# Edge softmax: turning the sum of s_i and mask by a round trip through DRAM and VectorE, one step ahead

## The chip, the cores and the metric

The kernel runs on one core of one Trainium2 chip. The metric is the device time of one execution in microseconds. A core has TensorE (PE: matrix products, and PEld for its weight loads), VectorE (DVE), ScalarE (ACT), GpSimd (POOL) and SyncE (SP), which here issues nearly all DMAs. Each engine works through its own list of instructions in order.

## The reference

Two layers of attention over a graph run on 128 batches of 128 tokens with 512 features. Layer 0 is masked attention with eight heads, and layer 1 is a graph attention whose scores are a sum of two numbers, s_i and s_j, under the same mask:

```python
def _L1_gnn_ref(h, W, a, adj):
    Wh = jnp.matmul(h, W)
    s_i = Wh @ a1
    s_j = Wh @ a2
    e = _leaky(s_i[:, :, None] + s_j[:, None, :])
    e = jnp.where(adj > 0, e, -9e15)
    attention = jax.nn.softmax(e, axis=1)
    h_prime = jnp.einsum('bij,bjf->bif', attention, Wh)
    return _leaky(h_prime)

x = _layernorm(x + _L0_gnn_ref(x, adj, Wq, bq, Wk, bk, Wv, bv, Wo, bo))
x = _layernorm(x + _L1_gnn_ref(x, W, a, adj))
```

The softmax of layer 1 runs over axis 1, the index i. So the tile of scores, made with i on the partitions, has to be turned to bring j onto the partitions and i along the free axis.

## The kernel before

Everything is float32. The batches are taken in groups of four for the products with Wq, Wk and Wv (`products`, each a Strassen scheme of seven part products), in pairs for those with Wo (`LayerZero`) and W (`LayerOne`), and singly for the softmax of layer 0 (`Softmax`) and for layer 1's attention (`Edge`).

One loop runs over steps t = -3 to 123, and then a written plan (`PLAN`) issues what is left of the last batches. In step t the kernel makes layer 0's softmax of batch t, its attention with V of batch t-1, a part of a group's products (`group()`), a pair's products (`pair()`: LayerZero at odd t, LayerOne of batches t-6 and t-5 at even t), and works on the edge softmax of the batches some seven behind. The order of the instructions on each engine is the order in which the code issues them; nothing reorders them.

Seven part products make a Strassen block, in the order of `ORDER`: ("p1", "t0"), ("p5",), ("p6", "t2"), ("p2", "c11"), ("p7", "t3", "c22"), ("p4", "c21"), ("p3", "c12"). Each call of `pair()` or `group()` takes one of these entries. p1, p6, p7 and p4 add into one PSUM bank ("y"), p5 and p3 into "w", and p2 has "x". t0, t2 and t3 are copies of "y" as it stands at that moment, made by ScalarE (pr_t for pairs, L456; st_t for groups, L341 and L345), so the next product into "y" must wait for the copy. c11 and the others are the finished blocks. For LayerOne they are written to `WH` (wh, L770 on VectorE and L768 on ScalarE), whose last column in each half holds s_i (half 0, c11 for the even batch and c21 for the odd one) and s_j (half 1).

The Edge of batch b goes through these methods:

- `sender()` (L796, ScalarE): e = mask + s_i, from the mask tile mf and a column of WH. At the end of step t it is made for batch t-6.
- `turn()` (L800, TensorE): e is turned with the identity into the PSUM tile p_e. It is called in the next step, behind the scores, the softmax's maxima and one `group()`.
- `add()` (L803, ScalarE): s_j is added while the tile is read from PSUM, and e is written back.
- `maxima()` (L808, L810, VectorE), `exp()` (L814, ScalarE), `divide()` (L818, L819, VectorE), then `product()` (p_h, L824, TensorE), `copy()`, `residual()`, `stats()`, `rstd()` (L648 and L650 on GpSimd), `apply()` (L663) and `store()` (L848, SyncE).

In the same step ScalarE makes eight exponentials of layer 0's softmax (`sm.exp`, L550) and eight divides (`sm.divide`, L564); VectorE makes the reciprocals between (`sm.reciprocals`, rs, L560). The middle of the step reads:

```python
            sm.exp(7)
            edge.divide()
            pair()
            sm.reciprocals(1)
            sm.divide(0, 1, 2, 3)
            group()
            sm.divide(4, 5)
            pair()
            sm.divide(6, 7)
```

Then `sm.spread()` writes pa to DRAM (pa_dram, L570) and, once it has landed, fetches it in four pieces as paz (L576), so that blocks of 32 by 32 stand where a transpose of such blocks on VectorE (paT, L585) makes the whole turn. SyncE also fetches batches in blocks (xz, L238), the masks (adj, L487), the residuals (L254) and the weights of V (wv_n, L405, a ring of three buffers), and sends x1 to DRAM (x_dram, L714). On GpSimd, `sum_x` forms the sums xS (L273 to L276) of a group's x at every fourth step, t divisible by 4.

Of the kernel before, what the change touches and what calls it, by code (L numbers as in the profile page):

```python
# [8 lines left out]
F32 = mybir.dt.float32  # L9
# [15 lines left out]
def kernel(  # L25
# [59 lines left out]
    nc = tc.nc  # L85
    B, P, D = x.shape
# [9 lines left out]
    small = ctx.enter_context(tc.tile_pool(name="small", bufs=3))  # L96
    dram = ctx.enter_context(tc.tile_pool(name="dram", bufs=3, space=bass.MemoryType.DRAM))
# [42 lines left out]
    def load_blocks(*args, **kwargs):  # L140
        for load in block_loads(*args, **kwargs):
            load()
# [4 lines left out]
    def right_blocks(t):  # L147

        return [
            lambda: nc.vector.tensor_sub(t[2], t[2], t[0]),  # L150
            lambda: nc.vector.tensor_sub(t[5], t[3], t[2]),
            lambda: nc.vector.tensor_sub(t[4], t[5], t[0]),
            lambda: nc.vector.tensor_sub(t[6], t[1], t[5]),
        ]

    def places(w):
        return [w[:, n] for n in range(7)]

    def columns(w):
        return w[:, 0:2], w[:, 2:4]  # L160
# [72 lines left out]
    def spread(src):  # L233

        z = work.tile([P, 4, P], F32, name="xz", bufs=3)
        block = src.rearrange("(a i) (q e) -> q i a e", i=32, q=4)
        for q in range(4):
            nc.sync.dma_start(z[32 * q : 32 * q + 32], block[q])  # L238
        return z
# [11 lines left out]
    def load_residual(b):  # L251

        X1[b] = work.tile([P, D], F32, name="x1", bufs=7)
        nc.sync.dma_start(X1[b], x[b])  # L254
# [230 lines left out]
    def load_mask(b):  # L485
        MF[b] = small.tile([P, P], I32, name="adj", bufs=2)
        nc.sync.dma_start(MF[b], adj[b])  # L487
# [9 lines left out]
    class Softmax:  # L497
# [27 lines left out]
        def add(self, r):  # L525
            if r == 0:
                self.pa = self.tile("pa", [P, 4, H, 32])
            by_head = self.pa.rearrange("p b h k -> p h b k")
            mf = MF[self.b].rearrange("p (b k) -> p b k", b=4)
            nc.vector.tensor_add(  # L530
                by_head[:, r * NC : (r + 1) * NC],
                self.lg[r].rearrange("p c (b k) -> p c b k", b=4),
                mf.unsqueeze(1).to_broadcast([P, NC, 4, 32]),
            )
# [31 lines left out]
                )  # L566

        def store(self):
            self.d = dram.tile([P, 4, H * 32], F32, name="pa_dram")
            nc.sync.dma_start(self.d, self.pa.rearrange("p b h k -> p b (h k)"))  # L570

        def fetch(self):
            self.paz = self.tile("paz", [P, 4, H * 32])
            block = self.d.rearrange("(a i) b e -> b i a e", i=32)
            for k in range(4):
                nc.sync.dma_start(self.paz[32 * k : 32 * k + 32], block[k])  # L576

        def spread(self):

            self.store()  # L580
            self.fetch()

        def transpose(self):
            self.paT = self.tile("paT", [P, H, P])
# [194 lines left out]
    class Edge:  # L779
# [18 lines left out]
        def turn(self):  # L798
            self.p = psum("p_e")[:, :P]
            nc.tensor.transpose(self.p, self.e, ident)  # L800

        def add(self):
            nc.scalar.activation(self.e, self.p, AF.Identity, bias=self.s[:, 1, :])  # L803

# [46 lines left out]
    def on(b):  # L851
        return 0 <= b < B
# [14 lines left out]
    none = Nothing()  # L867
# [16 lines left out]
    sm = fin = edge = coming = none  # L884
# [66 lines left out]
    END = B - GROUP  # L951

    first_homes = {"pa": lambda shape: work.tile(shape, F32, name="pa", tag="x1T")}
    for t in range(-3, END):
        pair_steps = []
        if t % GROUP == 1 and on(t + 3):
            rest = group_steps
            group_steps, v_pieces, fetch_v = products((t + 3) // GROUP)
            group_steps = rest + group_steps
        if t % 2 == 1 and on(t - 3):  # L960
            pair_steps = zero[(t - 3) // 2] = LayerZero((t - 3) // 2)
            pair_steps = pair_steps.steps()
        if t % 2 == 0 and on(t - 6):
            pair_steps = LayerOne((t - 6) // 2).steps()

        def group(n=1):
            for _ in range(min(n, len(group_steps))):
                group_steps.pop(0)()
            for _ in range(min((3 if t == -3 else 2 if t >= 1 else 1) * n, len(chores))):
                chores.pop(0)()  # L970

        def w1_chores(n):
            for op in [w1_sums.pop(0) for _ in range(n)]:
                op()

        def pair(n=1):
            for _ in range(min(n, len(pair_steps))):
                pair_steps.pop(0)()

        if on(t + 1):  # L980
            load_mask(t + 1)
        if t == 0:
            load_blocks(Wo, columns(wo), nc.sync, spread_rows=False)
            late_chores = right_blocks(places(wo)) + load_bias()
        if t == 1:
            w1_loads, w1_sums = load_w1()
            for chore in late_chores:
                chores += [w1_loads.pop(0), chore]
            chores += w1_loads

        last, sm = sm, Softmax(t, first_homes if t in (0, 2, 4) else None) if on(t) else none
        sm.scores()
        if t % 2 == 1 and on(t - 3):
            zero[(t - 3) // 2].by()
            zero[(t - 3) // 2].bw()
        if later and t > 4:
            later.pop().go_back()
        if t == 5:
            group(2)
        if t < 3:  # L1000
            sm.maxima()
            group(2)
            if on(t - 2):
                load_residual(t - 2)
            if t == 0 and on(GROUP):
                sum_x(1)()
            sm.exp(0, 1, 2, 3)
            last.transpose()
            group()
            sm.reciprocals(0)  # L1010
            sm.exp(4, 5, 6, 7)
            if t == 1:
# [4 lines that stand above are left out]
            sm.divide(4, 5, 6, 7)  # L1017
            if t == 1:
                group()
            if on(t + 1):  # L1020
                mask_float(t + 1)
        elif t == 4:

            layer = later.pop()
            sm.maxima()
            group()
            layer.apply(0)
            load_residual(2)
            if on(8):
                sum_x(2)()  # L1030
            sm.exp(0, 1)
            group()
            sm.exp(2, 3, 4, 5)
            last.transpose()
            group()
            layer.store(1)
            layer.store(0)
            layer.fetch(1)
            layer.fetch(0)
            sm.exp(6, 7)  # L1040
            group()
            sm.reciprocals(0)
            sm.reciprocals(1)
            sm.divide(0, 1, 2, 3, 4, 5, 6, 7)
            mask_float(5)
        else:
            sm.maxima()
            group()
            if t == 5:
                turn_x1(4)  # L1050
                x1_sums()
            edge = coming
            edge.turn()
            edge.add()
            fin.residual()
            if on(t - 2):
                load_residual(t - 2)
            edge.maxima()
            fin.stats()
            fin.rstd()  # L1060
            x1_sums()
            if t % GROUP == 0 and on(t + GROUP):
                sum_x(t // GROUP + 1)()
            pair()
            sm.exp(0, 1, 2, 3)
            edge.exp()
            pair()
            sm.exp(4, 5)
            last.transpose()
            group()  # L1070
            sm.reciprocals(0)
            pair()
            sm.exp(6)
            fin.apply()
            fin.store()
            sm.exp(7)
            edge.divide()
            pair()
            sm.reciprocals(1)
            sm.divide(0, 1, 2, 3)  # L1080
            if t == 3:
                w1_chores(4)
# [4 lines that stand above are left out]
            if on(t + 1):  # L1087
                mask_float(t + 1)
            group()
            if t in (3, 5):  # L1090
                w1_chores(4 if t == 3 else 8)
        sm.spread()
        for b in x_turns(t):
            transpose_x(b)
        for b in x_turns(t + 1):
            load_x(b)
        if on(t + 1):
            mask(t + 1)
        pair(2)
        if t % 2 == 0 and on(t - 6):  # L1100
            turn_x1(t)
        if t not in (0, 4):
            group(21 if t % GROUP == 0 else 1)
        coming = Edge(t - 6) if on(t - 6) and t + 1 < END else none
        coming.sender()
        fin = edge
        fin.product()
        fin.copy()

        last.attend()  # L1110
        last.copy()
        if t % 2 == 0:
            last.sum(0, 1, 2, 3)
# [183 lines left out]
```

## Time and profile before

| what | value |
|---|---|
| runs | 2420.37, 2423.23, 2420.54 us, median 2420.54 |
| profiled execution, own time | 2418.28 us |
| its span | 2416.5 us |
| mean granted TensorE clock | 0.998 |
| PE busy | 2374.0 us, 98% |
| DVE busy | 1802.4 us, 75% |
| ACT busy | 1521.9 us, 63% |
| POOL busy | 812.7 us, 34% |
| DMA queue of SP | 350448 packets, 376.60 MB, 48.8% of 16 engines |
| p_e on PE (L800) | 117 in the loop of 273 ns each, 11 in the plan |
| a step from its first score product to the next one's | about 18.0 us; 19.7 us where t is divisible by 4 |

A line of instructions names the source line, engine, operation, the tiles as out<-in, shapes and count. A busy time is the time in which at least one such instruction runs; matmuls overlap, so the record of one is longer than its share of the engine. "Idle before" is time in which the engine stood still just ahead of the instruction, with what ended it. The chain of waits follows the end of the run back, at each step to what released the instruction.

### The profile page before, as it was taken

The page shows a single profiled execution, that of the slowest core. Times are in us where ns is not written, and L with a number is a line of the kernel's source. Part 1 is how long each engine was busy: PE and PEld are TensorE (multiplying, and loading weights), DVE is VectorE, ACT ScalarE, POOL GpSimd, SP SyncE. Part 2 cuts the span into 40 slices and gives each one's busy share as a digit, 9 for nine tenths or more (in the row PEclk, how much of TensorE's full clock was granted, in tenths as well). Part 3 has the DMA queues.
Part 4 walks back from the last instruction along what each step waited for, and adds up shares of the span by engine and source line. Part 5 has one row for each costly group of instructions (what it writes and reads, how often), then busy time and mean ns, then how long its engine had stood idle before and what let it go on. Part 6 is the DMA issues. An engine that isn't in the chain of part 4 may idle for free.

```text
span 2416.5 us, 43217 instructions
## 1 busy us (share of the span) xinstructions
PE 2374.0 (98%) x13467; PEld 1984.4 (82%) x13467; DVE 1802.4 (75%) x3602; ACT 1521.9 (63%) x5463; POOL 812.7 (34%) x1195
## 2 busy tenths in 40 slices
PE   8899999999999999999999999999999999999996
PEld 7788888888888888888888888888888888888874
DVE  4677787777777777877877777778778777777777
ACT  3566666666666666666666666666666666666685
POOL 1233333233343333332333433333323334333335
PEclk9999999999999999999999999999999999999999
DMA  6554544544545545445445445454454454554453
GB/s 193 176 159 144 168 154 151 178 147 148 170 149 165 163 145 166 148 157 175 142 152 169 152 162 169 136 170 148 160 169 148 153 171 142 166 169 139 149 165 101
DMA packets 351253, 379.88 MB, mean 157 GB/s; under 512 B 38952, under 2 KB 255024, under 8 KB 351024
## 3 DMA queue, kind: packets, MB, share of 16 engines
q1 hardware_dynamic: 350448, 376.60, 48.8%
q8 instruction: 108, 1.77, 0.3%
q14 instruction: 121, 0.99, 0.1%
q10 hardware_dynamic: 576, 0.52, 0.1%
HBM read 240.91 MB, written 136.05 MB: 156 GB/s over the span
## 4 chain that ended last, share of the span: by engine, by line
PE 89%; DMA 3%; DVE 2%; issue 2%; ACT 2%; POOL 1%; SPq 1%; DVEq 0%; POOLq 0%; ACTq 0%
PE st_y L364 26%; PE p_y L445 17%; PE st_w L364 13%; PE p_w L445 8%; PE st_x L364 6%; PE lg L516 5%; PE p_oT L598 5%; PE p_h L824 4%; PE p_x L445 4%; DMA pa_dram<-pa 1%; PE p_e L800 1%; DMA x_dram<-x 1%; DMA wv_n<-wv 0%; DMA paz<-pa_dram 0%; ACT pa L564 0%
## 5 line engine op out<-in xcount | busy, mean ns | idle before, releaser
L550 ACT ACTIVATE pa<-pa,nmax 128x128 f32<-128x128 f32 x1008 | 392.3, 393 | 12.2 <-DVE nmax L539 12.1
L648 POOL TENSOR_SCALAR ve<-mv 128x1 f32<-128x1 f32 x256 | 70.0, 273 | 865.1 <-DVE mv L644 856.6
L564 ACT ACTIVATE pa<-pa,rs 128x128 f32<-128x128 f32 x1008 | 331.0, 394 | 32.6 <-DVE rs L560 29.3
L530 DVE TENSOR_TENSOR pa<-lg,mf 128x512 f32<-128x512 f32 x252 | 162.0, 685 | 160.1 <-PE lg L516 158.3
L273 POOL TENSOR_TENSOR oS<-oT 128x256 f32<-128x256 f32 x63 | 45.8, 727 | 648.8 <-ACT oT L612 648.8
L341 ACT COPY st_t<-st_y 128x512 f32<-128x512 f32 x192 | 110.4, 575 | 154.7 <-PE st_y L364 154.7
L550 ACT ACTIVATION_READ_ACCUMULATOR pa<-pa,nmax 128x1 f32 x1008 | 192.4, 191 | 0.0
L345 ACT ACTIVATE st_t<-st_y,b_cols 128x256 f32<-128x256 f32 x192 | 80.6, 471 | 168.0 <-PE st_y L364 168.0
L650 POOL TENSOR_TENSOR rstd<-ve,mhalf 128x1 f32<-128x1 f32 x256 | 177.0, 691 | 21.3
L598 PEld LDWEIGHTS p_oT<-paT,v 128*64 128x64 f32 x2016 | 107.5, 136 | 91.5 <-issue 91.0
L612 ACT ACTIVATE oT<-p_oT,b_cols 128x128 f32<-128x128 f32 x504 | 144.0, 368 | 55.0 <-PE p_oT L598 54.0
L456 ACT COPY pr_t<-p_y 128x257 f32<-128x257 f32 (+1 forms) x375 | 138.3, 369 | 53.3 <-PE p_y L445 49.6
L585 DVE STREAM_TRANSPOSE paT<-paz 128x1024 f32<-128x1024 f32 x126 | 156.8, 1245 | 15.5 <-DMA paz<-pa_dram 14.3
L539 DVE TENSOR_REDUCE nmax<-pa 128x8 f32<-128x1024 f32 x126 | 153.7, 1220 | 4.4
L516 PE MATMUL lg<-kT,qT 64*128 64x128 f32 x2048 | 148.7, 285 | 0.0
L516 PEld LDWEIGHTS lg<-kT,qT 64*128 64x128 f32 x2048 | 124.2, 187 | 22.9 <-issue 22.9
L598 PE MATMUL p_oT<-paT,v 128*64 128x128 f32 x2016 | 137.9, 279 | 0.0
L445 PE MATMUL p_y<-wo,oT 128*128 128x256 f32 x504 | 129.8, 380 | 1.4 <-ACT pr_t L456 0.8
L445 PE MATMUL p_y<-w,x1S 128*128 128x257 f32 x496 | 128.0, 380 | 1.9 <-ACT pr_t L456 1.9
L445 PE MATMUL p_y<-wo,oS 128*128 128x256 f32 x504 | 129.4, 379 | 0.0
L445 PE MATMUL p_y<-w,x1T 128*128 128x257 f32 x496 | 128.5, 381 | 0.2 <-DVE x1T L243 0.2
L364 PE MATMUL st_y<-xT,wq 128*128 128x256 f32 x512 | 125.8, 389 | 2.5 <-DMA wq<-in_L_gnn_Wq_dram 2.5
(202 smaller groups left out, 5952.1 us busy)
## 6 DMA issues: line engine op xcount, KB each, us to landing
pa_dram<-pa SPq DMA_DIRECT2D x126, 512.0 KB, 2.6
paz<-pa_dram SPq DMA_DIRECT2D x504, 128.0 KB, 2.6
wv_n<-wv SPq DMA_DIRECT2D x224, 256.0 KB, 2.9
x<-in_x_dram SPq DMA_DIRECT2D x128, 256.0 KB, 2.9
x_dram<-x SPq DMA_DIRECT2D x128, 256.0 KB, 2.6
xz<-x_dram SPq DMA_DIRECT2D x512, 64.0 KB, 2.0
xz<-in_x_dram SPq DMA_DIRECT2D x496, 64.0 KB, 2.1
out_dram<-z SPq DMA_DIRECT2D x120, 256.0 KB, 2.5
```

The costliest lines, as they stand in the source:

```text
L364: nc.tensor.matmul(p[:, m, :], lhs, rhs, start=start and m == 0 and kc == 0, stop=True, skip_group_check=True,)
L445: nc.tensor.matmul(p[:, :width], xs()[n][:, kc, :], w[:, PLACE[n], kc, :], start=start and kc == 0, stop=True, skip_group_check=True,)
L456: nc.scalar.copy(t[:, :width], p[:, :width])
L516: nc.tensor.matmul(self.lg[r][:, c, :], q[rows, c, cols], k[rows, c, cols], start=c == 0, stop=True, skip_group_check=True,)
L530: nc.vector.tensor_add(by_head[:, r * NC : (r + 1) * NC], self.lg[r].rearrange("p c (b k) -> p c b k", b=4), mf.unsqueeze(1).to_broadcast( ...
L539: nc.vector.tensor_reduce(self.nmax, by_head, AX.XY, ALU.max, negate=True)
L550: nc.scalar.activation(self.pa[:, :, h, :], self.pa[:, :, h, :], AF.Exp, bias=self.nmax[:, h : h + 1], accum_out=self.sums[:, h : h + 1],)
L564: nc.scalar.activation(self.pa[:, :, h, :], self.pa[:, :, h, :], AF.Copy, scale=self.rs[:, h : h + 1])
L585: nc.vector.transpose(self.paT.rearrange("p h (a i) -> p a h i", i=32), self.paz.rearrange("p a (h k) -> p a h k", k=32),)
L598: nc.tensor.matmul(self.oT[r * HD : (r + 1) * HD, c, :], v[:, h * HD : (h + 1) * HD], self.paT[:, r * NC + c, :], start=c == 0, stop=True, ...
L612: nc.scalar.activation(OT[pair][:, c, h * P : (h + 1) * P], self.oT[:, c, :], AF.Identity, bias=b_cols[:, 1, c : c + 1],)
L650: nc.gpsimd.tensor_tensor(self.r, ve, mhalf, ALU.pow)
```

## The change

`turn()` on TensorE is replaced, in the loop, by three methods. `store_sender()` writes e to DRAM. `fetch_sender()` reads it back in four pieces, each of 32 partitions by 4 by 32 elements, into a tile ez. `turn_blocks()` turns the blocks of 32 by 32 on VectorE into a tile e_turned, on which `add()` and `maxima()` then work.

The sender and the store are made in the middle of the step ahead, between `sm.reciprocals(1)` and the first divides. The four fetches are issued at the end of that step, between the store of pa and its fetches. The turn comes at the start of the next step, directly behind `sm.scores()`. The plan behind the loop keeps `turn()`.

```diff
         def store(self):
             self.d = dram.tile([P, 4, H * 32], F32, name="pa_dram")
             nc.sync.dma_start(self.d, self.pa.rearrange("p b h k -> p b (h k)"))
...
-        def spread(self):
-
-            self.store()
-            self.fetch()
...
             self.p = psum("p_e")[:, :P]
             nc.tensor.transpose(self.p, self.e, ident)
 
+        def store_sender(self):
+            self.d = dram.tile([P, P], F32, name="e_dram")
+            nc.sync.dma_start(self.d, self.e)
+
+        def fetch_sender(self):
+            self.ez = small.tile([P, 4, 32], F32, name="ez", bufs=2)
+            block = self.d.rearrange("(a i) (q e) -> q i a e", i=32, q=4)
+            for q in range(4):
+                nc.sync.dma_start(self.ez[32 * q : 32 * q + 32], block[q])
+
+        def turn_blocks(self):
+
+            self.e = self.p = small.tile([P, P], F32, name="e_turned", bufs=1)
+            nc.vector.transpose(self.e, self.ez.rearrange("p a e -> p (a e)"))
+
         def add(self):
             nc.scalar.activation(self.e, self.p, AF.Identity, bias=self.s[:, 1, :])
...
         sm.scores()
+        coming.turn_blocks()
...
             edge = coming
-            edge.turn()
             edge.add()
             fin.residual()
...
             edge.divide()
             pair()
             sm.reciprocals(1)
+            coming = Edge(t - 6) if on(t - 6) and t + 1 < END else none
+            coming.sender()
+            coming.store_sender()
             sm.divide(0, 1, 2, 3)
...
-        sm.spread()
+        sm.store()
+        if t >= 6:
+            coming.fetch_sender()
+        sm.fetch()
         for b in x_turns(t):
             transpose_x(b)
...
         if t not in (0, 4):
             group(21 if t % GROUP == 0 else 1)
-        coming = Edge(t - 6) if on(t - 6) and t + 1 < END else none
-        coming.sender()
         fin = edge
         fin.product()
         fin.copy()
```

## The prediction

> **What bounds the kernel now.** I read the page's busy shares first, then the chain of waits, then the timeline of single steps, because a share is an average and this change is worth what its own stage makes of it.
>
> ```profile
> PE 2374.0 (98%) x13467; PEld 1984.4 (82%) x13467; DVE 1802.4 (75%) x3602; ACT 1521.9 (63%) x5463; POOL 812.7 (34%) x1195
> ...
> PE 89%; DMA 3%; DVE 2%; issue 2%; ACT 2%; POOL 1%; SPq 1%; DVEq 0%; POOLq 0%; ACTq 0%
> ```
>
> TensorE is busy 98% of the span and is 89% of the chain. From 300 to 2200 us it waits for nothing but four late weight loads (the waits: 2.4 us on wv_n in all). So a product taken off PE pays in full, and a delay elsewhere costs only where it makes PE wait. The chain through step t = 56 (its first score product starts at 1053.65):
>
> ```profile
> 1056.72 0.11 PE p_e L800
> ...
> 1063.76 0.87 PE p_y L445 x4
> 1064.63 1.73 PE st_y L364 x8
> 1066.36 0.87 PE p_y L445 x4
> ```
>
> p_e takes 0.11 us; it has half the columns of an L445 product, so an eighth of a quartet's 0.87: 0.108. The quartets at 1063.76 and 1066.36 (p7 and p4 of LayerOne) add into the same bank, and between them ACT must copy it (pr_t, "t3"). So p4 is the deadline for ACT. The timeline of that place (start, length, engine, line; PE records start 0.17 us ahead of the chain's pieces):
>
> ```profile
> 1061.25 1.27 DVE L663 TENSOR_SCALAR z<-z,mv,rstd 128x512 f32<-128x512 f32 x1
> 1062.25 1.26 ACT L564 ACTIVATE pa<-pa,rs 128x128 f32<-128x128 f32 x4
> 1062.32 1.34 POOL L274 TENSOR_TENSOR xS<-xS,xT 128x512 f32<-128x512 f32 x1
> 1062.63 1.11 DVE L819 TENSOR_SCALAR att<-att,rt 128x128 f32<-128x128 f32 x1
> ...
> 1063.65 0.41 DVE L770 TENSOR_TENSOR wh<-p_x,pr_t 128x257 f32<-128x257 f32 x1
> 1063.79 0.32 SPq L405 DMA_DIRECT2D wv_n<-wv  x1
> ...
> 1064.19 0.69 ACT L564 ACTIVATE pa<-pa,rs 128x128 f32<-128x128 f32 x2 [0.67 <-DVE rs L560]
> ...
> 1064.79 0.35 ACT L456 COPY pr_t<-p_y 128x257 f32<-128x257 f32 x1
> ...
> 1066.19 1.03 PE L445 MATMUL p_y<-w,x1T 128*128 128x257 f32 x4
> ```
>
> The reader is to see three things. wh<-p_x (c11), which holds the s_i of the even batch, is ready only at 1064.06. ACT has by then done four divides. The t3 copy ends at 1065.14, 1.05 us before p4.
>
> **What the skill says.** The Trainium skill's Perfetto Trace Analysis (Tensor Engine Instruction) calls ACT's and DVE's queues "strict FIFO"; the trace agrees (the divides at 1064.19 idle 0.67 us for rs). SBUF — State Buffer (SBUF: two separate sides) says VectorE and GpSimd take their shared ports as an exclusive lock for a whole instruction; here L663 takes 1.27 us beside POOL's xS sums and 0.51 at 1008.10, and L819 1.11 against 0.29 at 1026.37. VectorE: DVE Perf Modes (The three transpose paths) has VectorE turn 32x32 blocks only, which is why the tile goes through DRAM; its 311 ns is for bf16, so I use this trace's rows:
>
> ```profile
> L585 DVE STREAM_TRANSPOSE paT<-paz 128x1024 f32<-128x1024 f32 x126 | 156.8, 1245 | 15.5 <-DMA paz<-pa_dram 14.3 <-issue 0.7 <-PE p_oT L598 0.5
> ...
> L243 DVE STREAM_TRANSPOSE xT<-xz 128x512 f32<-128x512 f32 x124 | 83.6, 693 | 1.1 <-DMA xz<-in_x_dram 1.0
> ...
> L800 PE MATMUL p_e<-ident,e 128*128 128x128 f32 x117 | 31.9, 273 | 0.0
> ```
>
> **The parts.**
>
> (1) Removed: 117 p_e on PE, 117 x 0.108 = **-12.6 us**. The 11 edges of the written plan keep theirs. One bank request of eight per step also goes (five banks in rotation); in the new rotation every bank's last reader is at least half a step old, so I add no wait.
>
> (2) Added on DVE: 117 block transposes. From 1245 ns at 1024 elements and 693 at 512, 128 take about 0.28 us, 33 us in all. In odd steps they stand before a wait for the scores of 2.3 to 3.1 us; at t mod 4 = 0 in the 0.75 us that DVE idles at 1054.23 for POOL's rstd; at t mod 4 = 2 that wait is 0.15, so the scores' add comes about 0.13 later. None reaches PE: 0. Without this cover each would delay the softmax by 0.28, and the t2 and t3 copies behind it have over 0.4 us.
>
> (3) Added on SP: 5 issues a step. One of like size (adj, 64 KB) takes 0.43 us. The four fetches (1.75) stand between the pa_dram store and the paz fetches, where SP already waits for the store to land:
>
> ```profile
> 1012.15 0.33 SPq L570 DMA_DIRECT2D pa_dram<-pa  x1
> 1014.75 1.75 SPq L576 DMA_DIRECT2D paz<-pa_dram  x4
> ```
>
> 2.27 us idle there, so 0; without it the paz fetch would come 1.75 later, and paT has about 5 us. ez lands some 2 us after issue (small loads: 2.0 to 2.3), near 1016.3; DVE asks for it after 1018.7. The 15 MB more are 4% of 380 MB. store_sender waits for ACT's sender, and behind it on SP stand the wv_n fetch (1063.79) and the pa store. The wv_n would be issued about 1.3 us later and needs 2.9 to land; PE takes it at 1069.66, so 1.6 us remain: 0.
>
> (4) Moved on ACT: add() now reads SBUF instead of PSUM (att's exp, SBUF to SBUF, takes 398 ns, the add 369: +0.03), and its wait for p_e (97 us in 59 steps) was idle time that gave nothing: 0. The sender is what counts: 402 ns long, 0.30 from start to start (at 1016.63), it goes from the step's end, where nothing gains (ACT then waits for p_h), to ahead of the first four divides. At odd t its s_i is a step old: +0.30, of which ACT's waits (0.27 for st_y at 1009.86, 0.23 for rs at 1046.55) take nearly all; the margin to p4 there is 0.7. At even t it is a **new wait on DVE's c11**, and all divides and t3 stand behind it. At t mod 4 = 2, c11 ends 9.31 after the step's start, 0.3 after the first divide would begin: t3 ends about 0.5 later, of a margin of 1.15. At t mod 4 = 0, from the step's start: c11 ends at 10.43; DVE's work follows from the step ahead and does not come forward with PE's 0.11, so 10.54. Sender 10.57, divides from 10.87, four of 0.29 to 12.04, two more to 12.64, t3 copy to 12.99. PE could start p4 at 12.55 - 0.11 = 12.44; it starts 0.05 after the copy (the gap between a t3 copy's end at 93.77 and its product at 93.83), 0.60 late, and the quartet after a wait takes 1.13 instead of 1.03: **0.70 us lost**. Such steps are t = 8, 12, ..., 120: 29 x 0.70 = **+20.3 us**. Next in line, p3 waits for DVE's c22, which then ends 0.5 us ahead of it: nothing more.
>
> (5) The late wv_n waits (2.9 us in four of these steps, ahead of p4) would partly be hidden in the new stall: between -2.9 and 0; I take -1.5.
>
> Sum, against the profiled execution's 2418.3: -12.6 + 20.3 - 1.5 = +6.2, 2424.5. The runs' median is 2.3 higher, hence 2420.5 + 6.2 = **2427**.
>
> **Unknown sizes.** The stall is the step's most uncertain figure: each 0.1 us is 2.9 us. From 0.45 (c11 does come forward and the copy overlaps) to 0.95 (sender 0.1 dearer, lock held longer) gives 2419 to 2434. Landing times of 128-byte pieces aren't in the trace: from hidden (0) to a late wv_n in some steps (+6).
>
> **Rivals.**
> A, faster: the sender's wait never reaches PE. DVE's two stretched instructions are 1.6 us of c11's 10.43; if the moved work let them miss POOL's sums, c11 would be done before ACT asks. It decides where t3 is delayed by under 0.9 us. Then 2420.5 - 12.6 = 2408. Against: POOL's sums follow DVE's own statistics in this step, so they meet again.
> B, much slower: transport. ez late by over 2.5 us would hold the scores' add on DVE, or wv_n behind store_sender would hold PE, 0.5 us in each of 29 steps or more: 2442 and up. The 2 us landings and SP's idle time speak against it.
> C: the change doesn't do what it says (p_e still on PE): 2420. The code leaves no room for it.
>
> **Chances.** About 0.2% (4.8 us) can be told from no change, so under 2415.7 is faster and above 2425.4 slower. My case 0.68, split by the stall's size into 0.42 slower and 0.26 same; A 0.20, faster; B 0.12, slower. The range 2409 to 2437 leaves out most of B and the edge of A; my case alone is 2419 to 2434.
>
> **What would show it.** p_e down from 128 records to 11; a step about 0.11 shorter at t mod 4 = 1, 2, 3 and some 0.6 longer at 0; in the waits, PE p_y L445 for ACT pr_t near 29 times, ACT e for DVE wh (about 2 us) in the same steps; no DMA wait of DVE at e_turned. No PE wait at p4 makes A right; PE waits for wv_n, or DVE's for ez, make B right.

## The result, and the profile after

The changed kernel takes 2422.36 us, median of four runs (2419.32 to 2424.92), beside 2421.16 for the kernel before (four runs): a ratio of **1.0003, 95% interval 0.9986 to 1.002**. No difference can be told. The profiled execution is 2420.01 us against 2418.28, its span 2418.1.

The page of the changed kernel: busy shares, then the chain by engine.

```profile
PE 2368.3 (98%) x13350; PEld 1975.1 (82%) x13350; DVE 1827.5 (76%) x3719; ACT 1515.2 (63%) x5463; POOL 812.7 (34%) x1195
...
PE 78%; ACT 9%; DVE 5%; DMA 3%; issue 2%; POOL 1%; SPq 1%; POOLq 0%; DVEq 0%; ACTq 0%
```

TensorE lost its 117 products, yet its share of the chain fell from 89% to 78%, and what it gave up went to ScalarE and VectorE: the end is now reached over them in part. Where that happens is seen in the chain through the same step as before, t = 56, whose first score product starts at 1053.92 (start, length, what):

```profile
1053.99 1.09 PE lg L516 x16
...
1058.18 1.65 ACT pa L550 x8
...
1061.48 0.13 DVE rs L560
1061.62 1.19 DVE z L659
...
1062.92 1.10 DVE att L830
1064.02 0.35 DVE wh L766
...
1064.38 0.40 ACT e L792
1064.79 1.75 ACT pa L564 x6
1066.54 0.27 ACT pr_t L456
...
1066.85 1.14 PE p_y L445 x4
```

Read it upwards from the last line. p4 (p_y) waits for the t3 copy (pr_t), the copy stands behind six divides, the divides behind the sender (e L792), and the sender waits for c11 (wh L766) on VectorE. Before c11 VectorE has two instructions whose records are 1.27 and 1.10 us long (z L659, att L830). In the chain before, PE alone filled this stretch. The timeline adds the idle time in brackets, and the SP queue:

```profile
1063.94 0.41 DVE L766 TENSOR_TENSOR wh<-p_x,pr_t 128x257 f32<-128x257 f32 x1
1064.38 0.40 ACT L792 ACTIVATE e<-mf,wh 128x128 f32<-128x128 bf16 x1 [1.86 <-DVE wh L766]
1064.69 1.85 ACT L564 ACTIVATE pa<-pa,rs 128x128 f32<-128x128 f32 x6
1064.81 0.32 SPq L800 DMA_DIRECT2D e_dram<-e  x1
1065.22 0.38 SPq L405 DMA_DIRECT2D wv_n<-wv  x1
...
1066.45 0.35 ACT L456 COPY pr_t<-p_y 128x257 f32<-128x257 f32 x1
...
1066.85 1.14 PE L445 MATMUL p_y<-w,x1T 128*128 128x257 f32 x4 [0.32 <-ACT pr_t L456]
```

ScalarE idles 1.86 us for c11 and passes the delay on: the four divides that used to fill that time now come after it. The 0.32 us in TensorE's bracket is not the whole loss, since the records of its products overlap and this quartet takes 1.14 us in place of 1.03; the loss is read from the length of the step.

I call a step the time from its first score product to the next step's. Its median length over t = 8 to 119, by t mod 4 = 0, 1, 2, 3, was 19.723, 17.960, 17.997, 17.960 us and is 20.197, 17.848, 17.885, 17.848. So 0.112 us is won in each of three steps and 0.474 lost in the fourth: a cycle of four is 0.14 us longer.

The waits of the whole run (engine, line, what it waited for; us in total, times, longest):

```profile
ACT e L792 <- DVE wh L766: 61.1, 57, 1.9
DVE e_turned L811 <- DMA ez<-e_dram: 46.8, 35, 3.0
...
PE p_y L445 <- ACT pr_t L456: 10.0, 27, 1.9
...
PE st_y L364 <- DMA wv_n<-wv: 3.3, 5, 1.0
```

The first and third are the predicted pair. The second was predicted not to be there. Most of it (40.7 us in 23 waits) stands at the start of the steps with t mod 4 = 3; the timeline around the start of t = 55 (1036.07) shows why it costs nothing:

```profile
1027.96 0.32 SPq L800 DMA_DIRECT2D e_dram<-e  x1
...
1030.56 0.32 SPq L571 DMA_DIRECT2D pa_dram<-pa  x1
1030.97 3.42 SPq L806 DMA_DIRECT2D ez<-e_dram  x4
...
1035.27 1.73 SPq L577 DMA_DIRECT2D paz<-pa_dram  x4
1036.04 0.31 DVE L811 STREAM_TRANSPOSE e_turned<-ez 128x128 f32<-128x128 f32 x1 [1.84 <-DMA ez<-e_dram]
...
1037.26 1.29 DVE L530 TENSOR_TENSOR pa<-lg,mf 128x512 f32<-128x512 f32 x2 [0.91 <-PE lg L516]
```

VectorE waits 1.84 us for ez. But after the turn it waits another 0.91 for the scores: the late turn used up idle time.

Why ez is late differs. In the step shown the four fetches take 3.42 us to issue, the longest of the 28 ends of a step with t mod 4 = 2 (median 1.77). In 24 of the 28 they begin late instead: the first fetch has to wait until the e_dram store has landed. SP's own waits from 300 to 2200 us, first before, then after the change:

```profile
SPq L576 <- DMA pa_dram<-pa: 297.4, 103, 5.0
```

```profile
SPq L806 <- DMA e_dram<-e: 33.7, 27, 2.5
SPq L577 <- DMA pa_dram<-pa: 22.7, 28, 1.7
```

Where t mod 4 = 2 the e_dram store lands 3.9 us after its issue, elsewhere 1.8 to 1.9 us (medians of the stores whose landing the profile gives). The two lines on pa_dram show that the fetches of ez now fill most of the time in which SP used to wait for that store.

### The profile page after: what moved, and what is told of

It is laid out like the page before. It is cut to its first block, busy times and chain, and to the rows that moved or that the text cites. A ratio compares the mean times of both kernels' runs of the same rounds, so it can differ in the third digit from the quotient of the medians.

```text
span 2418.1 us, 44124 instructions
## 1 busy us (share of the span) xinstructions
PE 2368.3 (98%) x13350; PEld 1975.1 (82%) x13350; DVE 1827.5 (76%) x3719; ACT 1515.2 (63%) x5463; POOL 812.7 (34%) x1195
## 3 DMA queue, kind: packets, MB, share of 16 engines
q8 instruction: 107, 1.75, 0.3%
## 4 chain that ended last, share of the span: by engine, by line
PE 78%; ACT 9%; DVE 5%; DMA 3%; issue 2%; POOL 1%; SPq 1%; POOLq 0%; DVEq 0%; ACTq 0%
PE st_y L364 22%; PE p_y L445 15%; PE st_w L364 12%; PE p_w L445 7%; PE lg L516 5%; PE p_oT L594 5%; PE st_x L364 4%; PE p_h L835 4%; PE p_x L445 3%; ACT pa L550 3%; ACT pa L564 3%; DMA pa_dram<-pa 1%; DVE z L659 1%; DVE att L830 1%; DMA x_dram<-x 1%
## 5 line engine op out<-in xcount | busy, mean ns | idle before, releaser
L530 DVE TENSOR_TENSOR pa<-lg,mf 128x512 f32<-128x512 f32 x252 | 162.0, 684 | 99.0 <-PE lg L516 98.3
L766 DVE TENSOR_TENSOR wh<-p_w,pr_t 128x257 f32<-128x257 f32 x122 | 51.8, 425 | 129.8 <-ACT pr_t L456 84.3
```

Source lines behind the costliest of these rows:

```text
L530: nc.vector.tensor_add(by_head[:, r * NC : (r + 1) * NC], self.lg[r].rearrange("p c (b k) -> p c b k", b=4), mf.unsqueeze(1).to_broadcast( ...
```

## The experiments

All were timed beside runs of the kernel before on the same chip (2419.16, 2419.44 and 2421.20 us in the three groups), and their ratios are to those; the first two rows of the table are the result above. "Step 0" is the median length at t mod 4 = 0; the other three are 17.848, 17.885, 17.848 in every kernel without p_e in the loop, but for the two with doubled fetches.

| kernel | median us | ratio, 95% interval | step 0 | c11 ends | t3 copied |
|---|---|---|---|---|---|
| before | 2421.16 | 1 | 19.723 | 10.43 | 11.51 |
| the change | 2422.36 | 1.0003 (0.9986 to 1.002) | 20.197 | 10.43 | 12.87 |
| no turn in the loop | 2403.78 | 0.9942 (0.993 to 0.9955) | 19.612 | 10.43 | 11.50 |
| sender early, turn on PE | 2430.58 | 1.0049 (1.0036 to 1.0062) | 20.256 | 10.43 | 12.93 |
| sender behind t3 | 2408.22 | 0.9953 (0.9939 to 0.9967) | 19.612 | 10.43 | 11.50 |
| sums behind the sender | 2420.35 | 1.0006 (0.9998 to 1.0014) | 20.196 | 10.43 | 12.87 |
| sender behind four divides | 2406.86 | 0.9946 (0.9934 to 0.9959) | 19.612 | 10.44 | 11.71 |
| apply behind the sender | 2407.29 | 0.9949 (0.9936 to 0.9961) | 19.612 | 9.02 | 11.47 |
| sums first | 2428.13 | 1.0038 (1.0025 to 1.005) | 20.423 | 10.66 | 13.10 |
| fetch doubled | 2510.44 | 1.038 (1.0354 to 1.0407) | 22.281 | 10.75 | 13.19 |
| fetch doubled in three steps of four | 2448.00 | 1.0111 (1.0097 to 1.0125) | 20.522 | 10.75 | 13.20 |
| the last version | 2405.84 | 0.9942 (0.9929 to 0.9956) | 19.612 | 10.44 | 11.71 |

c11 and t3 are in us from the start of a step with t mod 4 = 0, medians of t = 8 to 116. The lengths of steps, here and below, come from the one profiled execution of each kernel.

**The two halves of the change, apart.** First the gain alone: the kernel before, without the turn in the loop, neither on TensorE nor elsewhere.

```diff
+        def skip_turn(self):
+            self.p = self.e
...
-            edge.turn()
+            edge.skip_turn()
```

> The kernel before without the turn in the loop: s_j is added to the tile as it stands, so the edge softmax of the loop is of another matrix. It prices p_e alone. Both theories: 117 products of 0.108 us, -12.6 us, about 2408 us, ratio 0.995. If PE's time has an end elsewhere, less than that.

It gave 2403.78 us, 15.4 less than the kernel before beside it. Then the cost alone: the kernel before with its sender early and its turn still on TensorE.

```diff
             sm.reciprocals(1)
+            coming = Edge(t - 6) if on(t - 6) and t + 1 < END else none
+            coming.sender()
             sm.divide(0, 1, 2, 3)
...
-        coming = Edge(t - 6) if on(t - 6) and t + 1 < END else none
-        coming.sender()
```

> The kernel before with one part of the change alone: the sender is made in the middle of the step ahead, the turn stays on PE, nothing goes through DRAM. Theory (the early sender's wait for c11 holds the ACT queue): p4 starts 0.05 us after a t3 copy that ends 12.87 us after the step's start instead of at 12.55, with 0.10 for the refill some 0.47 us in each of 29 steps, +13.6, less up to 2.6 us of late weight loads hidden in it: about 2432 us, ratio 1.005. Rival (the transport is the cost): as before, 2421.

It gave 2430.58, 11.4 more, with step 0 longer by 0.53 and no other step changed. So the change holds a gain of some 15 us and a loss of some 11, in different steps. They don't simply add up (-4.0 against +1.2 for the change). The late wv_n fetches lengthen some of the steps with t mod 4 = 0 beyond their median, in all by 3.7 us before; the gain alone saves 2.3 of that, the cost alone all 3.7, the change 2.6. And with the turn gone as well the stall is 0.585 us, not 0.53. In the profiled executions these two make 3.4 and 1.5 us, most of what is missing.

**The sender put back in one step of four.** The change, with the sender behind the t3 copy at t mod 4 = 0 alone:

```diff
             sm.reciprocals(1)
-            coming = Edge(t - 6) if on(t - 6) and t + 1 < END else none
-            coming.sender()
-            coming.store_sender()
+            if t % GROUP:
+                coming = Edge(t - 6) if on(t - 6) and t + 1 < END else none
+                coming.sender()
+                coming.store_sender()
...
             sm.divide(4, 5)
             pair()
+            if t % GROUP == 0:
+                coming = Edge(t - 6) if on(t - 6) and t + 1 < END else none
+                coming.sender()
+                coming.store_sender()
```

> The changed kernel, but at every fourth step (t divisible by 4) the sender and its store come after the t3 copy instead of ahead of the divides. Theory (ACT waits for c11 there, and t3 and PE's p4 stand behind it, 0.58 us in each of 29 steps): the stall at p4 goes, the p_e saving of 12.6 us stays whole, about 2408 us, ratio to before 0.995, and those steps take 19.6 us. Rival (the round trip through DRAM and the turn on VectorE eat the gain): as the changed kernel, about 2422, ratio 1.000.

2408.22: as the theory said, with step 0 at the 19.612 us of the kernel that has no turn in its loop. The whole stall is in those 29 steps. One step (t = 31) was 2.03 us longer, with one wait of VectorE for ez of 5.3 us in the trace.

**Is it the wait, or what is queued behind it?** The sender still ahead of t3 and still waiting for c11, but with four divides ahead of it:

```diff
             sm.reciprocals(1)
+            if t % GROUP == 0:
+                sm.divide(0, 1, 2, 3)
             coming = Edge(t - 6) if on(t - 6) and t + 1 < END else none
             coming.sender()
             coming.store_sender()
-            sm.divide(0, 1, 2, 3)
+            if t % GROUP:
+                sm.divide(0, 1, 2, 3)
```

> The change, with the sender and its store made behind the first four divides in place of ahead of them, in the steps with t divisible by 4 alone. The sender still waits for c11, but the four divides no longer stand behind it. Theory (what costs is the work queued behind the wait, not the wait): divides from about 8.6, sender at 10.46 after c11, the last two divides ahead of t3 from 10.76, t3 copied by about 11.7, PE at p4 not held: 2406 to 2411 us, ratio 0.994 to 0.996, with ACT's wait for wh shorter (about 0.7 us in place of 1.9 where the divides fill it). Rival (any place of the sender ahead of t3 costs the stall, since it occupies ACT there): 2414 to 2424 us.

2406.86. The timeline of its step t = 56 (first score product at 1048.76):

```profile
1057.26 1.27 ACT L564 ACTIVATE pa<-pa,rs 128x128 f32<-128x128 f32 x4
...
1058.77 0.41 DVE L766 TENSOR_TENSOR wh<-p_x,pr_t 128x257 f32<-128x257 f32 x1
1059.22 0.40 ACT L792 ACTIVATE e<-mf,wh 128x128 f32<-128x128 bf16 x1 [0.69 <-DVE wh L766]
1059.53 0.68 ACT L564 ACTIVATE pa<-pa,rs 128x128 f32<-128x128 f32 x2
...
1060.11 0.35 ACT L456 COPY pr_t<-p_y 128x257 f32<-128x257 f32 x1
...
1061.20 1.03 PE L445 MATMUL p_y<-w,x1T 128*128 128x257 f32 x4
```

The sender starts 10.46 us into the step, exactly as in the change (1064.38 - 1053.92 = 10.46), and p4 waits for nothing. The four divides, 1.27 us, now lie in what was idle time. What cost was the queue behind the wait.

**Why is c11 late?** The chain names two stretched instructions of VectorE. One of them was moved away, behind the sender, in these steps:

```diff
-            fin.apply()
-            fin.store()
+            if t % GROUP:
+                fin.apply()
+                fin.store()
...
             coming.store_sender()
+            if t % GROUP == 0:
+                fin.apply()
+                fin.store()
```

> The change, with LayerNorm's apply (L659 of the changed kernel, z) and its store made behind the sender in the steps with t divisible by 4 alone. That takes an instruction of 1.27 us, stretched beside POOL's xS sums, from ahead of c11 on DVE. Theory (the sender waits for c11, and c11 for DVE's stretched instructions, so the stall at p4 is DVE's time ahead of c11): c11 ends near 9.2 to 9.6 us after the step's start in place of 10.43, the t3 copy near 11.7, no wait of PE for pr_t, 0.58 us less in each of 29 steps: about 2405 to 2410 us, ratio 0.994 to 0.996. Rival 1 (c11 is held by PE's product p2 or by another instruction that moves into the place): c11 stays above 10.2 and the time as for the change, 2420 to 2424. Rival 2 (z made later holds the LayerNorm's next user): a new wait elsewhere, 2412 to 2420.

```profile
1054.87 0.41 DVE L766 TENSOR_TENSOR wh<-p_x,pr_t 128x257 f32<-128x257 f32 x1
...
1055.31 0.40 ACT L792 ACTIVATE e<-mf,wh 128x128 f32<-128x128 bf16 x1 [0.46 <-DVE wh L766]
```

c11 ended at 9.02, a little below what was expected, the wait of the sender fell from 1.86 to 0.46 us, and the time was 2407.29. So VectorE's order decides when c11 is ready, and TensorE's p2 does not hold it. Two more runs went for the cause of the stretching, POOL's sums xS. The first issued them in the code behind the sender:

```diff
-            if t % GROUP == 0 and on(t + GROUP):
-                sum_x(t // GROUP + 1)()
...
             coming.store_sender()
+            if t % GROUP == 0 and on(t + GROUP):
+                sum_x(t // GROUP + 1)()
```

> The changed kernel with GpSimd's sums of x (four instructions of 1.3 us at every fourth step) issued behind the sender instead of ahead of the exponentials. Theory (L659 and L830 on VectorE are stretched by 1.6 us beside these sums, which makes c11 late in just those steps): both fall to about 0.5 and 0.3 us, c11 ends near 8.9 us after the step's start, ACT waits 0.3 us or less for it, p4 is not held, about 2408 us, ratio 0.995. Rival (c11 is late for another reason, or the transport is the cost): as the changed kernel, 2422.

Nothing changed (2420.35), and the edit turned out to be void: POOL has nothing else between the two places, so its sums ran right behind rstd as before. The second put them where they had to run earlier:

```diff
+            if t % GROUP == 0 and on(t + GROUP):
+                sum_x(t // GROUP + 1)()
             sm.maxima()
...
-            if t % GROUP == 0 and on(t + GROUP):
-                sum_x(t // GROUP + 1)()
```

> The change, with POOL's sums xS of a group's x issued at the start of the steps with t divisible by 4, ahead of the softmax's maxima, in place of behind rstd; nothing else moves. POOL's idle time there is 5.9 us, the sums take about 5.2. Theory (DVE's two instructions ahead of c11 are stretched because they run beside POOL's sums): z (L659) falls from 1.27 to about 0.51 us and att's divide (L830) from 1.1 to about 0.29, c11 ends near 8.9 if nothing else is stretched, up to 10.2 if DVE's statistics are stretched in their stead; below about 9.95 the stall is gone and the time is 2405 to 2411 us, ratio 0.994 to 0.996. Rival (they are long for another reason, or the sums only stretch other instructions ahead of c11): c11 stays near 10.4 and the time is as for the change, 2419 to 2424; with rstd held up behind the sums it could be above that.

2428.13, against the theory's 2405 to 2411 and above the rival's 2419 to 2424. The timeline of its step t = 56 (first score product at 1058.13):

```profile
1058.70 1.27 POOL L273 TENSOR_TENSOR xS<-xT 128x512 f32<-128x512 f32 x1
1058.77 1.49 DVE L659 TENSOR_SCALAR x<-x,mv,rstd 128x512 f32<-128x512 f32 x1 [0.53 <-POOL rstd L646]
...
1060.17 1.28 DVE L530 TENSOR_TENSOR pa<-lg,mf 128x512 f32<-128x512 f32 x2
...
1062.69 1.74 POOL L276 TENSOR_TENSOR xT<-xT,xS 128x512 f32<-128x512 f32 x1
1063.34 1.64 DVE L846 TENSOR_TENSOR z<-z,x 128x512 f32<-128x512 f32 x1
...
1067.54 0.52 DVE L659 TENSOR_SCALAR z<-z,mv,rstd 128x512 f32<-128x512 f32 x1
1068.16 0.29 DVE L830 TENSOR_SCALAR att<-att,rt 128x128 f32<-128x128 f32 x1
```

The same four instructions of VectorE in the change (first score product at 1053.92):

```profile
1054.55 0.55 DVE L659 TENSOR_SCALAR x<-x,mv,rstd 128x512 f32<-128x512 f32 x1 [0.53 <-POOL rstd L646]
...
1058.29 0.69 DVE L846 TENSOR_TENSOR z<-z,x 128x512 f32<-128x512 f32 x1
...
1061.54 1.27 DVE L659 TENSOR_SCALAR z<-z,mv,rstd 128x512 f32<-128x512 f32 x1
...
1062.92 1.10 DVE L830 TENSOR_SCALAR att<-att,rt 128x128 f32<-128x128 f32 x1
```

Half of the theory held: without POOL beside them z takes 0.52 us in place of 1.27 and att 0.29 in place of 1.10. But, as the rival had it, the sums stretched two other instructions ahead of c11 in their stead, x (1.49, was 0.55) and z<-z,x (1.64, was 0.69). c11 came 0.23 us later than in the change, and step 0 was 0.23 longer: one for one. The adds from PSUM (L530, 1.28 us for two, 1.29 in the change) weren't stretched beside the same sums. This fits what the Trainium skill says in SBUF — State Buffer (SBUF: two separate sides): VectorE meets GpSimd's lock in a two-port mode or with two inputs from SBUF, and not otherwise. z<-z,x has two such inputs; in which mode x, z and att ran, the trace doesn't tell.

**Is the transport free?** The four small fetches were made a second time, into a DRAM tile that nobody reads:

```diff
                 nc.sync.dma_start(self.ez[32 * q : 32 * q + 32], block[q])
+            again = dram.tile([4, 32, 4, 32], F32, name="ez_again")
+            for q in range(4):
+                nc.sync.dma_start(again[q], block[q])
```

> The change, with the four small-piece reads of each step's e_dram made a second time, from DRAM to a DRAM tile that nobody reads, on SP's queue right behind the first four and ahead of the paz fetches. SP has four more issues of about 0.43 us per step, 1.7 us, and the queue 1024 more packets of 128 B per step. Theory (the turn's transport is hidden under SP's wait for the pa_dram store and under DVE's slack): as the change, 2420 to 2424 us, ratio to the kernel before 1.000 to 1.001; paT on DVE may come up to 1.7 us later without reaching PE. Rival (the transport costs time, and what the change lacks against its own sum is paid there): at least 5 us more than the change, 2427 or above, with more DMA waits of DVE at e_turned or at paT and of PE at wv_n.

2510.44, 91 us more than the kernel before. The theory is out; the rival's "2427 or above" holds, by far more than it named. (The second fetch added 576 packets a step, not 1024.) SP's queue in its timeline at the end of step t = 55 (step 56 starts at 1090.07):

```profile
1085.10 0.32 SPq L571 DMA_DIRECT2D pa_dram<-pa  x1
1085.51 2.15 SPq L806 DMA_DIRECT2D ez<-e_dram  x4
1087.70 2.47 SPq L809 DMA_DIRECT2D ez_again<-e_dram  x4
1090.21 3.11 SPq L577 DMA_DIRECT2D paz<-pa_dram  x4
...
1093.90 0.38 SPq L405 DMA_DIRECT2D wv_n<-wv  x1
```

paz is fetched 5.1 us after its store in place of the 2.6 of the kernel before, and the next step's first wv_n fetch is issued 3.8 us into the step (2.8 in the median of such steps), against 0.35 in the change. In all TensorE then waits 61.0 us for wv_n (30 times). SP's wait for the store had 2.27 us to spare, and the first four fetches had already taken 1.75 of them. So this run doesn't say that one fetch costs time, but that a second one finds no room. In the next the second fetch was left out at t mod 4 = 3 alone (the edit is set against the doubled fetch, and shown in part):

```diff
-            for q in range(4):
+            for q in range(4 if twice else 0):
                 nc.sync.dma_start(again[q], block[q])
...
-            coming.fetch_sender()
+            coming.fetch_sender(t % GROUP != 3)
```

> The doubled fetch of the turn (four more issues of small pieces on SP ahead of the paz fetch), in the steps with t mod 4 = 0, 1 and 2 alone; at t mod 4 = 3 the fetch is made once. Doubled in every step it took 91 us more than the kernel before. Theory (SP's queue has room for the second fetch in all steps but this one, where it pushes the wv_n fetches of the next step back by 3 us): the waits of PE for wv_n go nearly back to those of the change, and the time to 2420 to 2432 us, the rest being ez waits on DVE at t mod 4 = 3 (7 us in the doubled run). Rival (the small pieces load the DMA engines themselves, in whatever step they are made): three quarters of the 88 us stay, 2480 us or more.

2448.00: between the two, and outside both. The waits of that kernel:

```profile
DVE e_turned L815 <- DMA ez<-e_dram: 105.9, 35, 5.5
...
PE st_y L364 <- DMA wv_n<-wv: 5.1, 8, 1.1
```

The wv_n part went as the theory said, from 61.0 to 5.1 us: it came from that one place in SP's queue, and the small pieces of the other three steps hardly touch it. The rest was priced too low: VectorE's waits for ez (111.8 us in the fully doubled kernel) stayed. They come from SP's queue as well. The second fetch at the end of a step with t mod 4 = 1 puts back all that SP issues in the step behind it, and the e_dram store goes out 2.6 us later than in the change. It lands as long after its issue as there (3.9 us, medians), but the turn of the next step comes 2.1 us later. That exceeds VectorE's slack at t mod 4 = 3 (those steps are 0.55 us longer) and puts VectorE back in the step that follows (c11 ends 0.33 later than in the change, and step 0 is 0.33 longer). 28 x (0.55 + 0.33) = 25 us, which is what is left.

**The last version** has the sender behind the first four divides at t mod 4 = 0, and in all steps the store to e_dram behind the group() that follows, so that the wv_n fetch goes ahead of it on SP. The edit is set against the version with the sender behind four divides.

```diff
             coming.sender()
-            coming.store_sender()
...
             group()
+            coming.store_sender()
             sm.divide(4, 5)
```

> The version with the sender behind the first four divides at t divisible by 4, and in every step store_sender issued behind the group() that follows, so that on SP the wv_n fetch of that group stands ahead of the e_dram store. Theory (nothing but a late wv_n separates that version from the kernel without p_e, 2403.8 us): late wv_n costs 0 to 2 us in all, 2403 to 2406 us, ratio 0.993 to 0.995. Rival (e_dram is then stored too late for ez, 2 us to land, and paz comes later): DVE's waits for ez grow, 2407 us or more.

2405.84, 0.9942 (0.9929 to 0.9956). It beats both kernels by 0.6%, and can't be told from the kernel without a turn in the loop (0.9942). It can't be told from the version without the later store (0.9946) either, so that edit is not shown to give anything.

## Why the prediction was right in mechanism and some 4 us too high

The predicted place, engines, cycle and signs are what the traces show, and the time fell in the range. But the likeliest case was a loss over 0.2%, and no change can be told. On the profiled execution the sum said +6.2 us and +1.7 was measured.

(1) p_e off TensorE, -12.6: **right**. Steps without the stall are 0.112 us shorter (0.108 predicted), and the kernel without a turn in the loop shows 0.111 or 0.112 in every step of the cycle.

(2) The turn on VectorE, 0: **right**. It took 305 ns where 280 was estimated; the Trainium skill's 311 ns for bf16 (VectorE: DVE Perf Modes, The three transpose paths) would have been nearer. With the stall away, all four steps have the lengths of the kernel with no turn in the loop.

(3) SP and the DMAs, 0: **right in the sum, wrong in one sign to look for**. The sentence "no DMA wait of DVE at e_turned" failed: 46.8 us of such waits are there. Two terms failed. The landing of the e_dram store, which the first fetch must await, was put at nothing: at the end of steps with t mod 4 = 2 it takes 3.9 us, so the fetches begin 1.6 us behind the pa_dram store in place of 0.4 (medians). And "DVE asks for it after 1018.7" was read from the start of t = 54 alone, where VectorE is ready 1.0 us into the step; where t mod 4 = 3 it is ready 1.9 us ahead of the step's start. The landing of the fetches themselves held (2.2 us in the median). VectorE's idle time ahead of the scores, named there as cover, held too. The cover of 2.27 us on SP was real, but nearly used up, as the doubled fetch showed; at t mod 4 = 2 the paz fetch already goes out 0.7 us later than before.

(4) The sender, +20.3: **right mechanism, mis-sized**. The failing term is "DVE's work follows from the step ahead and does not come forward with PE's 0.11, so 10.54". c11 ends at 10.43 with and without p_e. VectorE waits for TensorE's scores in every odd step, so it comes forward with TensorE, and c11 keeps its distance from the scores of its own step. With 10.43 in place of 10.54 the same working gives the t3 copy at 12.88 (measured 12.87) and a stall of 0.59. Measured: 20.197 - 19.612 = 0.585, so 29 x 0.585 = 17.0 us, 3.3 less. The start 0.05 after the copy held (12.87 to 12.93).

(5) The late wv_n waits, -1.5: the excess of steps over their median at t mod 4 = 0 was 3.7 us before and is 1.1 now: **-2.6**. That is one execution of each kernel; in the other kernels without p_e in the loop, the two with doubled fetches apart, it lies between 0.8 and 4.3. So the size of this term is not told apart from chance.

With these, -12.6 + 17.0 - 2.6 = +1.8 for the +1.7 measured (+1.3 with the 0.112 us of (1)). Both mis-sizings went the same way, 4.4 us, about the width of what counts as no change.

Rival A named the right threshold (t3 is delayed by 1.36 us, more than its 0.9) and was wrong for this kernel, but the versions with the sender behind four divides and with apply moved are A: t3 delayed by 0.2 us or not at all, and 2407 us where A said 2408. B's transport stayed hidden in the change (where t mod 4 = 3, VectorE waits 1.5 us for ez in the median). With the second fetch in three steps of four that wait is 3.6 us, beyond B's 2.5, and 2448 us is what B describes. C is out: p_e has 11 records left.

## What to carry over

An instruction moved ahead in a strict queue takes its wait along, and what must be priced is the work behind it up to the next deadline: four divides that used to fill the wait were worth about as much here as the products taken off the bound engine. Ask whether the producer hangs on the bound engine: here it did, and came forward with it. And a cover is spent once: 2.27 us hid four issues, and four more in each step cost some 90 us.

## What the runs showed of the hardware that was not expected

- 117 tiles through DRAM and back in pieces of 128 bytes cost nothing measurable in the right place, but SP's issue of such a fetch varies: 0.43 us in the median of 468, 2.29 at most.
- An e_dram store of 64 KB lands 1.8 us after issue in the median, and 3.9 us in the steps with t mod 4 = 2. A pa_dram store of 512 KB lands after 2.6 us in the median, and after 4.6 us in the step shown above (issued 1030.56, landed 1035.2).
- POOL is stretched in its turn: xT<-xT,xS took 1.74 us, not 1.27, where z<-z (0.68 us) had started on VectorE just ahead of it. That one stretches the other is shown for these pairs alone.
